# Deformable attention and bottleneck on one Trainium2 core: a different order in the stretch before the first image's attention

## The chip, the cores and the metric

The kernel runs on one core of one Trainium2 chip. The metric is the device time of that core in microseconds. A core has five engines that run their own instruction queues and meet only at semaphores: TensorE (PE, with its weight loads PEld), VectorE (DVE), ScalarE (ACT), GpSimd (POOL) and SyncE (SP), which here issues most of the DMA transfers. Each queue is worked off in the order in which the program wrote it, so an instruction that waits holds back everything behind it on its own engine.

## The reference, cut to what matters

The input `x` is 8 images of 512 channels and 64 by 64 pixels, in fp32. Layer 0 is deformable attention on the group-normalised input, layer 1 a convolutional bottleneck on the group-normalised sum. The part that matters here is the beginning of layer 0:

```python
x = x + _L0_conv_ref(_gn(x), w_q, w_off1, b_off1, w_off2, w_kv, w_out, b_out)
...
q = einsum('oc,bchw->bohw', w_q, x)                 # 512 x 512 weights
t = gelu(oi[:, :, ::4, ::4] * w_off1 + b_off1)      # every 4th pixel of q
off = tanh(einsum('oc,bchw->bohw', w_off2, t)) * 4.0
kv_feats = grid_sample_bilinear(oi, vgrid)          # 256 points, gathered from q itself
k, v = split(einsum('oc,bchw->bohw', w_kv, kv_feats), 2)
attn = softmax(einsum('bhid,bhjd->bhij', q * scale, k))   # 8 heads of 64, 256 keys
```

So an image goes through statistics, normalisation, query projection `q`, offsets, a gather of 4 neighbours of each sample point out of `q`, the keys and values of the 256 sampled points, and then the attention proper.

## The kernel before, in words

**Tiling.** An image lies in SBUF as 8 tiles of 512 pixels; a tile is 128 partitions by 4 channel blocks by 512 pixels, 1 MB. `x_tile`, `q_tile` and `out_tile` are neighbouring places in one region, so `q` of tile t overwrites the place of x tile t-1. Two regions hold two images at a time.

**Statistics** (`norm_x`, `group_stats`, `norm_q`). `bn_stats` (L201) runs on DVE per tile and channel block as the tiles land. Then `group_stats` has a short chain with no other work beside it: 4 `bn_aggr` (L169, DVE), a product `gps` with the group matrix in `cst` (L173, PE), 4 small DVE instructions (L175 to L179), a second product `gpsb` (L182, PE), `ve` (L184, DVE) and the power -0.5 on POOL (L185). The functions are generators: every `yield` hands control back to the caller, who decides what is written into the queues in between. After that `normalise` (L217, L221) scales x in place: tile 0 on DVE, tile 1 on POOL, tiles 2 to 7 on ACT with the bias `shift` (L230).

**Query projection** (`project_q`). A Strassen-like scheme with 7 half-size products per tile replaces 8. The weight sums (`of_weights`, L253 to L259) and the pixel sums (`of_tile`, L264 to L270) are made on DVE. A `product` is 8 PE instructions (4 fp32 matmuls, two passes each) with 256 moving columns. Per tile the order is p1 and p2, p6, p7, p5, p4, p3, and after each the DVE additions that bring the result out of PSUM: p6 to L364 and p2 to L365, p7 to L372, p5 to L378, p4 to L385 and p5 to L386, p3 to L391. p1, p2 and p7, p4 sit in pairs of banks of pool `ps_s`; p6, p5, p3 take single banks of `ps_mm`, which has two, so each of them needs the bank of the second last user to be free. `by_pixel` (L324 to L335) transposes the finished tile before, copies it (`qr`) and stores it to DRAM (`qd`), from where it is gathered later. For the last tile there is no next tile to hide in: its four transposes come after the last product, their copies go to DVE (L332), and `qr` of image 1 has two buffers.

**Sampling** (`sample`). Offsets by 8 small products `po` for each half (L424, one bank of `ps_mm`), tanh on ACT (L433), some 25 small DVE instructions in three groups, and then 20 slots. 16 of the slots issue two indirect gathers on POOL each (L519); 8 of them, three slots after the first gathers of their half step, also weigh what has landed (L483 to L488, DVE); two transpose the finished features into channels (`to_channels`, L493 and L498, one bank of `ps_mm`).

**What sets the order here.** Everything inside `manual_schedule` is queued in program order. At the start: `load_x(0)`, `load_wq`, `load_x(1)` and more on SP; statistics and normalisation of image 0; `project_q` of image 0, into whose steps the statistics of image 1 are dealt. Then `project_q` of image 1 and `sample` of image 0 are interleaved (L1193 to L1200): each sampling step adds to `room` (6 for a slot, 2 for one of the three steps before), and steps of `project_q` are taken while `room` is positive, each subtracting the number it yields (4, 2.5, 2.5, 2.5, 2.5, 2 per tile). After that: the last four transposes of image 1 (`drain(other)`), `next(samples[1])` (the `po` products and tanh of image 1), the load of `wout`, `project_k(0)` (4 banks of 8 PE instructions, each scaled into `kt` by ACT at L540, then a maximum over `kt` on DVE, L546), the first `logits`, `project_v(0)` (L560), and the attention loop over 8 images of 8 tiles of 4 head pairs.

Of the kernel before, what the change touches and what calls it, by code (L numbers as in the profile page):

```python
# [8 lines left out]
F32 = mybir.dt.float32  # L9
I32 = mybir.dt.int32  # L10
AF = mybir.ActivationFunctionType
ALU = mybir.AluOpType
# [4 lines left out]
P = 128  # L17
# [5 lines left out]
TP = 512  # L23
NT = N // TP
# [25 lines left out]
def kernel(  # L50
# [15 lines left out]
    nc = tc.nc  # L66
# [8 lines left out]
    ps_a = ctx.enter_context(tc.tile_pool(name="ps_a", bufs=1, space=PSUM))  # L75
# [6 lines left out]
    wbuf = cpool.tile([P, NCC, TP], F32, name="wbuf")  # L82
# [18 lines left out]
    def x_tile(b, t):  # L101
        return spot(b, t + 1)
# [8 lines left out]
    ident = cpool.tile([P, P], F32, name="ident")  # L111
    make_identity(nc, ident)
    cst = cpool.tile([P, K_N], F32, name="cst")
    nc.sync.dma_start(cst, consts)
    vec = cpool.tile([P, V_N], F32, name="vec")
    nc.sync.dma_start(vec, vecs)
    nhalf = cpool.tile([P, NCC], F32, name="nhalf")
    nc.vector.memset(nhalf, -0.5)

# [14 lines left out]
    def load_wq():  # L134
        nc.sync.dma_start(wbuf, w_qT.rearrange("(cc p) o -> p cc o", p=P))
# [19 lines left out]
    def drain(*gens):  # L155
        for gen in gens:
            for _ in gen:
                pass
# [30 lines left out]
    LATE = 0.01  # L189
# [4 lines left out]
    def load_x(b, order=range(NT), queue=nc.sync):  # L194
        for t in order:
            queue.dma_start(x_tile(b, t), xs[place[b]][:, :, t * TP : (t + 1) * TP])
# [7 lines left out]
    def quarters(a):  # L204

        h = C // 2
        return [[a[:, 2 * i : 2 * i + 2, h * j : h * (j + 1)] for j in range(2)] for i in range(2)]

    def norm_q(b, st, norms):

        gs = yield from group_stats(st, 0, b)
        shift = small.tile([P, NCC], F32, tag="shift", name=f"shift_{b}")

        def normalise(t, cc):
            xc, scale = x_tile(b, t)[:, cc, :], gs[:, 1, cc : cc + 1]
            if t < 2:
                (nc.vector, nc.gpsimd)[t].tensor_scalar(  # L217
                    xc, xc, gs[:, 0, cc : cc + 1], scale, ALU.subtract, ALU.mult
                )
            else:  # L220
                nc.scalar.activation(  # L221
                    xc, xc, AF.Identity, bias=shift[:, cc : cc + 1], scale=scale
                )

        norms[b] = normalise
        yield None
        for t in (1, 0):
            for cc in range(NCC):
                normalise(t, cc)
        nc.vector.scalar_tensor_tensor(shift, gs[:, 0], -1.0, gs[:, 1], ALU.mult, ALU.mult)  # L230
        yield None

    def project_q(b, normalise, mq, qd, pools, sums, aside=None):

# [7 lines left out]
        s1, s2, s4, t1, t2_, first = sums  # L242
# [1 line left out]

        (w11, w21), (w12, w22) = quarters(wbuf)
        V = nc.vector

        def of_weights(n):

            if b == 1:  # L250
                return
            if n == 1:
                V.tensor_add(s1, w21, w22)  # L253
            elif n == 2:
                V.tensor_sub(s2, s1, w11)
            elif n == 3:
                V.tensor_sub(w21, w11, w21)
            else:
                V.tensor_sub(s4, w12, s2)  # L259

        def of_tile(t, n):
            (x11, x12), (x21, x22) = quarters(x_tile(b, t))
# [75 lines left out]
            )  # L338

        for n in range(1, 4):  # L340
            of_weights(n)
            of_tile(0, n)
        for t in range(NT):
            (x11, x12), (x21, x22) = quarters(x_tile(b, t))
            (q11, q12), (q21, q22) = quarters(q_tile(b, t))

            def pixels(k):

                if t:
                    by_pixel(t - 1, k)  # L350
                if t + 2 < NT:
                    normalise(t + 2, k)

            bank1, bank2 = two_banks(t, 0)
            p1 = product(bank1, w11, x11)
            p2 = product(bank2, w12, x21)
            nc.scalar.copy(q11, p1)
            of_tile(t, 4)
            if t:
                activate(t - 1)  # L360
            yield 4
            p6 = product(one_bank(t, 1), s2, t2_)
            pixels(0)
            V.tensor_add(q12, q11, p6)  # L364
            V.tensor_add(q11, q11, p2)  # L365
            if t == 0:
                of_weights(4)
            yield 2.5
            bank1, bank2 = two_banks(t, 2)
            p7 = product(bank1, w21, x12)  # L370
            pixels(1)
            V.tensor_add(q22, q12, p7)  # L372
            if aside and t in (3, 4):
                largest(2, t - 3)
            yield 2.5
            p5 = product(one_bank(t, 3), s1, t1)
            pixels(2)
            V.tensor_add(q12, q12, p5)  # L378
            if t + 1 < NT:
                of_tile(t + 1, 1)  # L380
                of_tile(t + 1, 2)
            yield 2.5
            p4 = product(bank2, w22, x21)
            pixels(3)
            V.tensor_add(q21, q22, p4)  # L385
            V.tensor_add(q22, q22, p5)  # L386
            if t + 1 < NT:
                of_tile(t + 1, 3)
            yield 2.5
            p3 = product(one_bank(t, 4), s4, x22)  # L390
            V.tensor_add(q12, q12, p3)  # L391
            if t == 2 and aside:
                aside()
            elif t + 1 < NT:
                largest(t, 0)
                largest(t, 1)
            yield 2
# [129 lines left out]
    def project_k(b, mq, w=None):  # L527

        feats = feats_of(b)
        for oc in range(NCC):  # L530
            pk = ps_mm.tile([P, TP], F32, tag="mm", name=f"pk_{b}_{oc}")
            for cc in range(NCC):
                nc.tensor.matmul(  # L533
                    pk[:, :NK],
                    (w[cc // 2][:, cc % 2] if w else wbuf[:, cc])[:, oc * P : (oc + 1) * P],
                    feats[:, cc // 2, cc % 2, :],
                    start=(cc == 0),
                    stop=(cc == NCC - 1),
                )
            nc.scalar.mul(kt[:, oc, :], pk[:, :NK], SCALE)  # L540
        if w is None:
            load_wkv(1)

        if mq is not None:
            mk = small.tile([P, 2, NCC], F32, tag="mk", name=f"mk_{b}")
            nc.vector.tensor_reduce(  # L546
                mk[:, 0, :], kt, axis=AX.X, op=ALU.max, apply_absolute_value=True
            )
            nc.vector.tensor_reduce(
                mk[:, 1, :], mq.rearrange("p t c -> p c t"), axis=AX.X, op=ALU.max  # L550
            )
            nc.vector.tensor_mul(bounds[:, b, :], mk[:, 0, :], mk[:, 1, :])
# [17 lines left out]
    exps, sums = {}, {}  # L570

    def logits(b, t, hp):
        qt = q_tile(b, t)
        es = exps[b, t, hp] = []
        for kc in range(2):
            ps = ps_s.tile([P, 2, TP], F32, tag="s", name=f"ps_{b}_{t}_{hp}_{kc}")
            for a in range(2):
                r = DH * a
                for k in (0, DH):
                    nc.tensor.matmul(  # L580
                        ps[k : k + DH, a, :],
                        kt[r : r + DH, hp, kc * P + k : kc * P + k + DH],
                        qt[r : r + DH, hp, :],
                        start=True,
                        stop=True,
                    )
            e = free_es.pop(0)
            nc.scalar.activation(e, ps, AF.Exp)  # L588
            es.append(e)
# [515 lines left out]
    names = [(b, t, hp) for b in range(B) for t in range(NT) for hp in range(NCC)]  # L1105
    st1s, mqs = {}, {}
# [43 lines left out]
    norms = {}  # L1150
# [17 lines left out]

    with tc.manual_schedule():
        load_x(0)  # L1170
        load_wq()
        load_x(1)

        wkv = [es4[0:2], es4[2:4]]
# [5 lines left out]
        st = new_stats(0, 0)  # L1180
        drain(norm_x(0, st))

        shared = [wout[:, i, :].rearrange("p (k o) -> p k o", k=2) for i in range(3)]
        shared += [kt[:, 0:2, :], kt[:, 2:4, :], wout[:, 3, :]]
        drain(norm_q(0, st, norms))

        st = new_stats(0, 1)
        blocks, other = norm_x(1, st), norm_q(1, st, norms)
# [4 lines left out]
        other = make_q(1, shared)  # L1193
        next(other)
        rest.pop(0)()
        room = 0
        for step in samples[0]:
            room += 6 if step is None else 2
            while room > 0:
                room -= next(other, 6) or 6  # L1200
        drain(other)
        rest.pop(1)()
        next(samples[1])
        load_wout()
        project_k(0, mqs.pop(0), wkv[0])
        logits(*names[0])
        project_v(0, wkv[1])
        for g in range(len(names)):
            b, r = divmod(g, ROUNDS)
# [56 lines left out]
        b, t, st = B - 1, NT - 1, st1s.pop(B - 1)  # L1266
# [10 lines left out]
        for hp in range(NCC):  # L1277
            for a in range(2):
# [5 lines left out]
                    start=True,  # L1284
# [127 lines left out]
```

## Time and profile before

| | us |
|---|---|
| median of 3 runs (lowest, highest) | 3277.78 (3276.54, 3277.90) |
| the profiled execution, its own time | 3278.57 |
| its span, first to last instruction | 3276.8 |
| PE busy in the span | 3209.6 (98%) |
| DVE, ACT, POOL busy | 2325.3, 1188.6, 614.0 |

The stretch that the change touches, by busy time of the engines in stretches of 20 us:

| stretch, us | PE | DVE | ACT | POOL | what runs |
|---|---|---|---|---|---|
| 0 to 20 | 0.00 | 12.31 | 1.28 | 0.69 | x of image 0 lands, statistics |
| 20 to 40 | 7.46 | 16.68 | 0.68 | 7.84 | statistics end, first products |
| 40 to 140 | 100.00 | 88.27 | 40.98 | 3.75 | q of image 0 |
| 140 to 160 | 17.95 | 16.17 | 5.62 | 10.00 | end of q 0, start of q 1 |
| 160 to 260 | 97.60 | 81.67 | 37.62 | 31.94 | q of image 1, samples of image 0 |
| 260 to 280 | 17.80 | 7.79 | 3.65 | 0.00 | end of q 1, keys of image 0 |
| 280 to 300 | 19.43 | 4.28 | 9.87 | 0.00 | values, first attention rounds |

A row of the timeline reads: start, duration of the merged group, engine, line, operation, output, inputs, shape, how often; in brackets the idle time of the engine before it and what released it. PE busy is modelled from pipelined matmuls.

### The profile page before, as it was taken

Reading aid. Unit: us, or ns where it says so; the run is one execution under the profiler, and the core shown is the slowest. Engines: PE = TensorE matmul, PEld = TensorE weight load, DVE = VectorE, ACT = ScalarE, POOL = GpSimd, SP = SyncE. Lnnn points to the kernel's source line nnn. Section 1 sums busy time; section 2 is a strip of 40 time slices with the busy share of each in tenths; the row PEclk is TensorE's granted clock in tenths of the full one; section 3 lists DMA queues with packets and bytes.
Section 4 is the critical chain, followed back from the end, with each engine's and each line's share of the span. In section 5 each row is a group of like instructions: output and inputs, shape, how many; then the busy total and the mean of one; then the engine's idle time right before and its main releaser. Section 6 shows DMA issues by size and latency. Waiting matters only on the chain.

```text
span 3276.8 us, 46318 instructions
## 1 busy us (share of the span) xinstructions
PE 3209.6 (98%) x18256; PEld 1535.1 (47%) x18256; DVE 2325.3 (71%) x3781; ACT 1188.6 (36%) x1652; POOL 614.0 (19%) x579
## 2 busy tenths in 40 slices
PE   6999999999999999999999999999999999999997
PEld 5884223348332583326833267322763228533223
DVE  7884765787757868587775977669776687766565
ACT  2343333344333443234333443334432354332530
POOL 1130300140402304022040220303112040210301
PEclk9999999999999999999999999999999999999998
DMA  7232221572326623275332843238332482322713
GB/s 276 78 92 77 78 78 65 194 158 75 116 91 204 132 78 117 78 228 120 91 92 98 224 114 110 86 128 199 93 106 82 168 193 68 107 93 68 130 40 143
DMA packets 293858, 390.60 MB, mean 119 GB/s; under 512 B 18312, under 2 KB 157832, under 8 KB 293632
## 3 DMA queue, kind: packets, MB, share of 16 engines
q1 hardware_dynamic: 240352, 261.70, 24.4%
q0 software_dynamic: 53280, 125.86, 17.3%
q8 instruction: 145, 2.38, 0.3%
q14 instruction: 81, 0.66, 0.1%
HBM read 193.52 MB, written 192.94 MB: 118 GB/s over the span
## 4 chain that ended last, share of the span: by engine, by line
PE 94%; DVE 3%; issue 1%; ACT 0%; DMA 0%; SPq 0%; POOL 0%; ACTq 0%; DVEq 0%; POOLq 0%
PE pp L667 27%; PE pq L275 23%; PE ps L580 14%; PE pa L598 13%; PE pqt L324 4%; PE pn L625 4%; PE pk L533 2%; PE pv L560 2%; PE po L1003 2%; PE py L733 1%; DVE rn L638 1%; DVE image L1090 0%; PE po L424 0%; PE pu L930 0%; DVE st L201 0%
## 5 line engine op out<-in xcount | busy, mean ns | idle before, releaser
L667 PE MATMUL pp<-image,wout 128*64 128x512 f32 x3584 | 818.6, 599 | 0.2 <-DVE qr L332 0.2
L588 ACT ACTIVATE es<-ps 128x1024 f32<-128x1024 f32 x512 | 502.6, 1023 | 259.4 <-PE ps L580 209.0
L598 PE MATMUL pa<-es,vt 128*64 128x512 f32 x2048 | 489.1, 598 | 1.7 <-ACT es L588 1.7
L667 PEld LDWEIGHTS pp<-image,wout 128*64 128x64 f32 x3584 | 236.9, 136 | 541.1 <-issue 463.7
L275 PE MATMUL pq<-image,wbuf 128*128 128x256 f32 x2048 | 476.4, 381 | 3.3 <-DVE image L217 1.9
L519 POOL DMA_INDIRECT g<-qd,row x256 | 281.1, 1098 | 1056.0 <-DVE row L516 990.5
L580 PE MATMUL ps<-image,kt 64*64 64x512 f32 x3584 | 437.3, 602 | 0.3
L275 PEld LDWEIGHTS pq<-image,wbuf 128*128 128x128 f32 x2048 | 382.0, 191 | 56.1 <-issue 5.0
L676 DVE SCALAR_TENSOR_TENSOR image<-pp,vec,image 128x512 f32<-128x512 f32 x224 | 167.2, 746 | 333.0 <-PE pp L667 332.6
L605 ACT COPY image<-pa 128x512 f32<-128x512 f32 x224 | 132.1, 590 | 675.7 <-PE pa L598 675.7
L610 DVE TENSOR_TENSOR es<-es,es 128x1024 f32<-128x1024 f32 x256 | 311.0, 1215 | 71.4 <-PE pa L598 71.4
L598 PEld LDWEIGHTS pa<-es,vt 128*64 128x64 f32 x2048 | 137.4, 137 | 294.7 <-issue 274.8
L580 PEld LDWEIGHTS ps<-image,kt 64*64 64x64 f32 x3584 | 114.4, 132 | 307.4 <-issue 175.7
L334 ACT COPY qr<-pqt 128x512 f32<-128x512 f32 x224 | 131.2, 586 | 238.1 <-PE pqt L324 225.4
L638 DVE RECIPROCAL rn<-pn 128x512 f32<-128x512 f32 x63 | 211.3, 3354 | 7.7 <-PE pn L625 5.8
L651 DVE STREAM_SHUFFLE rb<-rn 128x512 f32<-128x512 f32 x252 | 184.6, 732 | 0.1
L185 POOL TENSOR_TENSOR gs<-ve,nhalf 128x4 f32<-128x4 f32 x15 | 15.6, 1042 | 895.6 <-DVE ve L184 895.6
L275 PE MATMUL pq<-es,es 128*128 128x256 f32 x768 | 181.5, 379 | 0.0
L1055 POOL DMA_DIRECT2D out_dram<-part x126 | 138.0, 1323 | 153.9 <-ACT part L1050 146.6
L201 DVE BATCH_NORM_STATS2 st<-image 128x6 f32<-128x512 f32 x256 | 159.2, 678 | 7.5 <-DMA image<-in_x_dram 7.3
L679 DVE BATCH_NORM_STATS2 st<-image 128x6 f32<-128x512 f32 x224 | 155.6, 694 | 7.7
L653 DVE TENSOR_TENSOR image<-image,rb 128x512 f32<-128x512 f32 x220 | 152.5, 693 | 7.6
(231 smaller groups left out, 3509.1 us busy)
## 6 DMA issues: line engine op xcount, KB each, us to landing
qd<-qr SPq DMA_DIRECT2D x256, 256.0 KB
image<-in_x_dram SPq DMA_DIRECT2D x112, 512.0 KB
out_dram<-image SPq DMA_DIRECT2D x49, 1024.0 KB
image<-in_x_dram POOLq DMA_DIRECT2D x48, 1024.0 KB, 10.3
out_dram<-part POOLq DMA_DIRECT2D x126, 256.0 KB, 7.2
image<-in_x_dram SPq DMA_DIRECT2D x16, 1024.0 KB
wbuf<-in_w_kvT_dram SPq DMA_DIRECT2D x14, 1024.0 KB
out_dram<-spare POOLq DMA_DIRECT2D x56, 256.0 KB, 8.0
```

What stands on the lines that cost most here:

```text
L201: nc.vector.bn_stats(st[:, cc, t, :], x_tile(b, t)[:, cc, :])
L275: nc.tensor.matmul(bank[:, o * 2 * P : (o + 1) * 2 * P], w[:, k, o * P : (o + 1) * P], xh[:, k, :], start=(k == 0), stop=(k == 1),)
L519: nc.gpsimd.indirect_dma_start(held[-1][:, i, :, :].rearrange("p j d -> p (j d)"), None, qd[:, :], bass.IndirectOffsetOnAxis(ap=row[:, ky, ...
L580: nc.tensor.matmul(ps[k : k + DH, a, :], kt[r : r + DH, hp, kc * P + k : kc * P + k + DH], qt[r : r + DH, hp, :], start=True, stop=True,)
L588: nc.scalar.activation(e, ps, AF.Exp)
L598: nc.tensor.matmul(pa[a * DH : (a + 1) * DH, :], vt[:, kc, hd * DH : (hd + 1) * DH], es[kc][:, a, :], start=(kc == 0), stop=(kc == 1),)
L610: nc.vector.tensor_add(es[0], es[0], es[1])
L638: nc.vector.reciprocal(rn, denominators.pop((b, t)))
L651: nc.vector.stream_shuffle(rb, rn, [2 * (hp % 2) + hp // 2] * 32)
L667: nc.tensor.matmul(pp[r : r + DH, :], wout[:, hp, oc * P + r : oc * P + r + DH], ao[:, hp, :], start=(hp == 0), stop=(hp == NCC - 1),)
L676: nc.vector.scalar_tensor_tensor(xt[:, oc, :], pp, col(V_BOUT + oc), xt[:, oc, :], ALU.add, ALU.add)
L679: nc.vector.bn_stats(st[:, oc, t, :], xt[:, oc, :])
```

## The change

It touches only what is queued before the attention loop. Six edits:

1. The loads of `cst` and `vec` move on SP from ahead of the eight loads of x to behind them, ahead of `load_wq`.
2. `of_weights` becomes a function of its own. For image 0, n = 1 is queued on DVE after the four small instructions of `group_stats`, and n = 2 after `ve`; n = 3 and 4 stay where they were. Image 1 makes none, as before.
3. `keep_up(5)` queues five fp32 products of `ident` with x tile 6 (512 columns) on PE ahead of `gps`, and `keep_up(2)` two more after `gpsb`; nothing reads their result.
4. `normalise` of image 0, tile 0, channel blocks 2 and 3 goes to ACT; `shift` is made between block 1 and block 2 of tile 0 rather than after block 3, for every image.
5. The dealing of samples: a slot now adds 4.5 and one of the three steps before it 5.
6. `project_q` of image 1 is run up to its mark `LATE` (before the last four transposes), then `project_k(0)` is queued, then the transposes, the maxima, `logits`, then `next(samples[1])`, the load of `wout` and `project_v(0)`.

```diff
     cst = cpool.tile([P, K_N], F32, name="cst")
-    nc.sync.dma_start(cst, consts)
     vec = cpool.tile([P, V_N], F32, name="vec")
-    nc.sync.dma_start(vec, vecs)
...
-            if t < 2:
+            if t == 1 or t == 0 and (b or cc < 2):
                 (nc.vector, nc.gpsimd)[t].tensor_scalar(
...
         for t in (1, 0):
             for cc in range(NCC):
+                if t == 0 and cc == 2:
+                    nc.vector.scalar_tensor_tensor(
+                        shift, gs[:, 0], -1.0, gs[:, 1], ALU.mult, ALU.mult
+                    )
                 normalise(t, cc)
-        nc.vector.scalar_tensor_tensor(shift, gs[:, 0], -1.0, gs[:, 1], ALU.mult, ALU.mult)
         yield None
+
+    def of_weights(n, sums):
+
+        s1, s2, s4 = sums[:3]
+
+        (w11, w21), (w12, w22) = quarters(wbuf)
+        if n == 1:
+            nc.vector.tensor_add(s1, w21, w22)
+        elif n == 2:
+            nc.vector.tensor_sub(s2, s1, w11)
+        elif n == 3:
+            nc.vector.tensor_sub(w21, w11, w21)
+        else:
+            nc.vector.tensor_sub(s4, w12, s2)
...
         for n in range(1, 4):
-            of_weights(n)
+
+            if b not in (0, 1) or (b == 0 and n == 3):
+                of_weights(n, sums)
             of_tile(0, n)
...
-            if t == 0:
-                of_weights(4)
+            if t == 0 and b != 1:
+                of_weights(4, sums)
...
         load_x(0)
+        nc.sync.dma_start(cst, consts)
+        nc.sync.dma_start(vec, vecs)
         load_wq()
...
-        drain(norm_q(0, st, norms))
+
+        idle = ps_a.tile([P, TP], F32, tag="pa", name="idle")
+
+        def keep_up(n):
+            for _ in range(n):
+                nc.tensor.matmul(idle, ident, x_tile(0, NT - 2)[:, 0, :], start=True, stop=True)
+
+        keep_up(5)
+        steps = norm_q(0, st, norms)
+        next(steps)
+        next(steps)
+        of_weights(1, shared)
+        next(steps)
+        of_weights(2, shared)
+        drain(steps)
+        keep_up(2)
...
         for step in samples[0]:
-            room += 6 if step is None else 2
+            room += 4.5 if step is None else 5
             while room > 0:
                 room -= next(other, 6) or 6
+        while next(other) != LATE:
+            pass
+        project_k(0, mqs.pop(0), wkv[0])
         drain(other)
         rest.pop(1)()
+        logits(*names[0])
         next(samples[1])
         load_wout()
-        project_k(0, mqs.pop(0), wkv[0])
-        logits(*names[0])
         project_v(0, wkv[1])
```

More of the change, by code (lines that the diff above doesn't have):

```diff
@@ L246, in project_q @@
         V = nc.vector
[L248 to L259, printed above, removed]
         def of_tile(t, n):
```

## The prediction

> **What bounds the kernel now.** I read the page's chain first, for the engine on which time counts.
>
> ```profile
> PE 94%; DVE 3%; issue 1%; ACT 0%; DMA 0%; SPq 0%; POOL 0%; ACTq 0%; DVEq 0%; POOLq 0%
> ```
>
> PE sets the end. So an edit is worth the PE idle time, or slow PE time, that it takes out of the first 300 us, provided PE stays the limit behind it; from about 290 us the attention loop is untouched and moves as a block. Next the timeline of the start (start, duration, group; in brackets idle time and releaser):
>
> ```profile
> 1.67 13.04 SPq L196 DMA_DIRECT2D image<-in_x_dram  x8
> ...
> 26.26 2.47 DVE L201 BATCH_NORM_STATS2 st<-image 128x6 f32<-128x512 f32 x4 [0.24 <-DMA image<-in_x_dram]
> ...
> 29.75 0.59 PE L173 MATMUL gps<-mv,cst 128*128 128x4 f32 x2 [29.75 <-DVE mv L169]
> ...
> 31.80 0.16 DVE L184 TENSOR_SCALAR ve<-gpsb 128x4 f32<-128x4 f32 x1 [0.68 <-PE gpsb L182]
> 32.05 1.03 POOL L185 TENSOR_TENSOR gs<-ve,nhalf 128x4 f32<-128x4 f32 x1 [30.74 <-DVE ve L184]
> 33.11 2.71 DVE L217 TENSOR_SCALAR image<-image,gs 128x512 f32<-128x512 f32 x4 [1.15 <-POOL gs L185]
> ...
> 33.72 5.56 PE L275 MATMUL pq<-image,wbuf 128*128 128x256 f32 x16 [1.95 <-DVE image L217]
> ...
> 39.12 1.89 PE L275 MATMUL pq<-kt,wout 128*128 128x256 f32 x8
> ```
>
> DVE follows the landing of x; then one chain runs to PE's first product. The 16 instructions of p1 and p2 take 39.12 - 33.72 = 5.40 us, where later groups of 8 follow each other by 1.73 us (0.216 each, so 3.46 for 16). In between they come every 0.427 us: PE starts at half speed. From 39.12 PE runs without a gap to 144. The same view later, only where PE waits between 160 and 290 us:
>
> ```profile
> 162.26 1.99 PE L275 MATMUL pq<-image,wbuf 128*128 128x256 f32 x8 [1.33 <-DVE spare L372]
> ...
> 221.62 1.99 PE L275 MATMUL pq<-image,wout 128*128 128x256 f32 x8 [1.06 <-DVE image L386]
> ...
> 264.99 1.99 PE L275 MATMUL pq<-image,wout 128*128 128x256 f32 x8 [0.77 <-ACT image L498]
> ...
> 272.06 2.90 PE L533 MATMUL pk<-image,es 128*128 128x256 f32 x8 [0.29 <-ACT pos L433]
> ...
> 275.44 5.91 PE L533 MATMUL pk<-image,es 128*128 128x256 f32 x24 [0.47 <-ACT kt L540]
> ...
> 283.16 7.13 PE L560 MATMUL pv<-es,image 128*128 128x512 f32 x16
> ...
> 290.22 1.94 PE L598 MATMUL pa<-es,vt 128*64 128x512 f32 x8
> ```
>
> And busy time in stretches (PE, PEld, DVE, ACT, POOL, then granted clock): the keys run while the clock is down.
>
> ```profile
> 272.00:276.00 4.00, 3.46 (x9) 2.38 (x10) 3.30 (x4) 0.40 (x2) 0.00 (x0) 0.62 0.62 149
> ```
>
> [...]0.427 against 0.216 us, with the turn about 3.6 us after 33.72. [...]after 15 transposes and 16 four-column products (267.77 to 271.8) the clock is 0.62. [...]tanh at 836.1 after the exp table's load at 827.99 and no further load until 1131.2. [...]L264 takes 1.09 us beside POOL at 36.4 and 0.69 later.
>
> **Start, step by step.** *Loads.* `cst` and `vec` are issued at 0.74 and 1.22, x at 1.67; x now goes at 0.74, 0.93 earlier. x stays limited by its transfer (a tile per 2.7 us), so the last tile lands at 25.33. Behind it come cst and vec (106 KB, an estimated 0.3 to 0.7 us at 385 GB/s or somewhat less), needed by `gps` at 28.82, and wbuf (2.7 us, by about 28.8), needed by n = 1 at about 30.0: covered by 1 to 3 us. SP issues wbuf at the same 14.75 as before, so later loads aren't late. -0.93.
> *Idle products.* Tile 6 lands at 22.62 (23.55 before). Five products are 10 instructions of 512 columns: 0.854 cold, 0.432 warm. With 3.6 us cold, 4.2 of them go cold and 5.8 warm: 6.1 us, end 28.7, against `gps` at 28.82. `gps` is queued right behind them; if the turn comes 0.7 us later it is late by about 0.3. Two more (4 x 0.432 = 1.73) fill 30.4 to 32.1, before the first product at 32.6.
> *Sums in the gaps.* n = 1 (0.68) on DVE covers the 0.68 in which `ve` waits for `gpsb`; with a warm PE `gpsb` returns sooner, so DVE becomes the last to end: together -0.16. n = 2 (0.68) lies in the 1.15 us of the power[...]: 0 to +0.6, no row shows the pair; I take +0.3 as the middle. Without it `normalise` starts at 32.02 (-1.09).
> *First products.* Blocks 0 and 1 on DVE end at 33.4, shift at 33.5, blocks 2 and 3 on ACT (2.93 / 4, about 0.75 each) at 34.3 and 35.0, where DVE had them at 35.8. p1 runs 32.63, waits for block 1, ends 34.7; p2 (block 3 for its second half) 36.43. `t1` and `t2_` on DVE end at 35.7 to 36.1. So p6 starts at 36.43: 39.12 - 36.43 = 2.69, minus 0.3 = **2.4**. Of it 1.9 is PE's clock and 0.9 the loads, less what the waits for blocks return. POOL's four of tile 1 (10.56 us) end by about 42.7; `of_tile(1, 2)` asks for them at 43.1, a cover of 0.4. For image 1 shift moves inside the same DVE sequence: 0.
>
> **Dealing.** Going through both lists of yields gives the order. *Tile 0*: before, the eight small instructions for `pos` (1.72 us on DVE) stood between p6's and p7's additions, and p4 waited for L372 1.33 us. Now they come after L372, which ends at 160.6 in the old clock, when p5 ends (160.8). The other small groups (1.3 and 1.0 us) now stand behind tile 0's p4 and tile 1's p1, p2; with them L372 of tile 1 ends at 174.4, just when p4 wants its bank: 0.15 lost. Gain 1.2. *Transposes to channels*: before, both stand between p4 and p3 and take p3's bank in turn, so that p3 waits for L386 (1.06) and for L498 (0.77). Now they stand after tile 4's p6 and tile 6's p7; the next to take a bank is p5, whose bank is free since L364. Gain 1.06 + 0.77 = 1.83; their own 0.47 each only moves. *Denser gathers*: from second gathers to weighing there are now 7.5 to 11 units of 0.87 us. Row cast behind other DVE work, two gathers (1.25 each), and landing
>
> ```profile
> DMA to landing us min/median/max: 2.4/2.7/3.4
> ```
>
> leave 0.1 to 2 us on the narrowest (half steps 5 and 6), and DVE has 0.4 us to p4's bank after that. Cost 0 to 0.5, taken 0. DVE carries 9.9 us per tile (11 x 0.69 + 2.35) and at most 3 us of sampling in 13.97. **3.0** in all.
>
> **Keys ahead.** Before: last p3 ends at 264.99 + 1.99 = 266.98; first `pa` at 290.22: 23.24 us. After, from the end of p3: keys 32 x 0.216 = 6.91, warm and without the waits (ACT scales a bank within 0.4, two banks ahead); transposes 4 x 0.47 to 8.8; logits 1.95 to 10.75; po 1.96 to 12.7. `pv` then needs the `ps_mm` bank of the last transposes. On DVE the maximum over `kt` is queued ahead of the copies and waits for the fourth scaling: 7.35 + 1.22 + 0.2 + 0.16 = 8.95; copies at 8.95 and 9.65; the third and fourth wait for the stores of the first two (about 2.45 from copy's end to release, as from 269.2 to 271.67): the fourth ends at 13.5. `pv` starts at 13.55 and takes 7.06: 20.6. Gain 23.24 - 20.6 = **2.6**. exp and kt are done long before. The four stores and the loads of wbuf and wout behind them on SP go out within 1 us of where they did; `wout` is wanted at 321.9 and the gathers of image 1 at 325.
>
> **Sum.** 2.4 + 3.0 + 2.6 = 8.0 us. The profiled execution would have 3278.57 - 8.0 = 3270.6 with a span of 3268.8; it lies 0.79 above the median of the runs, so the median becomes 3277.78 - 8.0 = 3269.8. What a measurement of this kernel can tell from no change is 0.2%, 6.56 us: faster means below 3271.2.
>
> **Rivals.**
> 1. *The clock falls in the moved tail.* [...]if the clock is down for pv, 3.6 us at half speed cost 1.8, and logits a few tenths: the tail gives 0.5, in all 5.9: 3271.9. For it: 272 to 276 above. Against: 1.95 us of logits stand between, and each quiet stretch is shorter than the 4 us that brought the clock down. The same total comes if the fuller DVE takes back the 1.2 of tile 0 and part of the waits for banks.
> 2. *Idle products too long.* All five cold are 8.54 us, from 22.62 to 31.16; `gps` is 2.34 late, two more cold ones take 3.41 us to about 36.3, and p6 starts at 41.7: a loss of 2.6 instead of 2.4 gained: 3274.8. Against: the first dense stretch turned after 3.6 us.
> 3. *Slower: DVE waits for gathers.* `weigh` stands ahead of the additions on DVE; if landing takes over some 5.5 us instead of 2.7, each of eight costs PE about 1.85, 14.8 in all, against 8.0 gained: 3284.6. It decides from 14.6 us, the gain and 6.6 more. Against: 3.4 at most so far, and the DMA engines are 0.23 to 0.41 busy from 160 to 260.
> 4. *The change does less because the gain is paid back later.* PE has no wait for DMA or x of later images in its chain, so I see no place and give it no chance of its own.
>
> **How the numbers follow.** Forecast 0.60, its own range 3268.3 to 3271.6, about 0.04 of it above the bound; rival 1 0.22; rival 2 0.10; rival 3 0.05; a little more gain (no wait for pv's bank[...]: 9.2, 3268.6, and less) 0.03. Faster 0.56 + 0.03 = 0.59; same 0.04 + 0.22 + 0.10 = 0.36; slower 0.05. The range takes in the forecast and rival 1 with its bounds and leaves out rivals 2 and 3: 3267.0 to 3274.5.
>
> **What would show it.** x's first issue at 0.74; `normalise` at about 32.2 and p6 at about 36.7; no PE wait on L372 in tile 0 of image 1 and none on L386 or L498; keys in 6.9 us with clock 1.00; first `pa` near 282.2 in place of 290.22. It is wrong if `gps` starts after 29.5, if L483 waits for DMA, or if pv's instructions come every 0.85 us.

## The result, and the profile after

| | before | after |
|---|---|---|
| median, us (lowest, highest; 20 runs each) | 3277.77 (3276.15, 3279.37) | 3272.61 (3267.79, 3273.63) |
| profiled execution, own time | 3278.57 | 3273.27 |
| its span | 3276.8 | 3271.5 |

The ratio is 0.9982, with a 95% interval of 0.9976 to 0.9988: 5.16 us less in the median, where 8.0 were forecast. The time lies inside the range on record, but under the 0.2% that was set as the bound of faster. The runs after spread over 5.8 us, those before over 3.2 here and over 6.2 in a later set of 39 (3273.76 to 3279.95), so the spread need not come from the change.

The gain is best read at three places: the start of p6 of image 0, the start of the last p3 of image 1, and the first `pa` of the attention loop.

| from, to (start of the PE group) | before | after | gained | forecast |
|---|---|---|---|---|
| 0 to p6 of image 0 | 39.12 | 37.59 | 1.53 | 2.4 |
| p6 of image 1 to its last p3 | 155.51 to 264.99: 109.48 | 153.98 to 259.60: 105.62 | 3.86 | 3.0 |
| last p3 of image 1 to first `pa` | 264.99 to 290.22: 25.23 | 259.60 to 285.34: 25.74 | -0.51 | 2.6 |
| together | 290.22 | 285.34 | 4.88 | 8.0 |

(Between p6 of image 0 and p6 of image 1 nothing moved: 155.51 - 153.98 is again 1.53.) The other 0.4 us of the span's 5.3 lie behind the first `pa`, where nothing was changed; what makes them up stays open. The page of the changed kernel still names PE:

```profile
PE 95%; DVE 3%; issue 1%; ACT 1%; DMA 0%; POOL 0%; SPq 0%; ACTq 0%; DVEq 0%; POOLq 0%
```

**Start.** The timeline of the changed kernel, to be laid beside that of before (L194 answers to L196, L171 to L173, L183 to L185, L215 to L217, L277 to L275):

```profile
0.74 12.17 SPq L194 DMA_DIRECT2D image<-in_x_dram  x8
...
22.31 6.04 PE L1196 MATMUL idle<-image,ident 128*128 128x512 f32 x10 [22.31 <-DMA image<-in_x_dram]
...
28.38 0.39 PE L171 MATMUL gps<-mv,cst 128*128 128x4 f32 x2
...
30.19 0.69 DVE L242 TENSOR_TENSOR wout<-wout,wbuf 128x512 f32<-128x512 f32 x1
30.31 1.46 POOL L183 TENSOR_TENSOR gs<-ve,nhalf 128x4 f32<-128x4 f32 x1 [29.00 <-DVE ve L182]
...
31.80 1.38 DVE L215 TENSOR_SCALAR image<-image,gs 128x512 f32<-128x512 f32 x2 [0.92 <-POOL gs L183]
...
33.32 1.28 ACT L219 ACT_TABLE_LOAD   x1 [33.32 <-DVE shift L228]
34.61 1.52 ACT L219 ACTIVATE image<-image,shift,gs 128x512 f32<-128x512 f32 x2
35.48 2.27 PE L277 MATMUL pq<-image,wbuf 128*128 128x256 f32 x8 [0.69 <-ACT image L219]
...
37.59 1.89 PE L277 MATMUL pq<-kt,wout 128*128 128x256 f32 x8
```

The statistics of the last tile start 1.37 us earlier, the short products return faster (`gps` takes 0.39 us instead of 0.59), the power on GpSimd takes 1.46 us instead of 1.03, and DVE starts to normalise at 31.80, 1.31 earlier. Then comes a line that was not there before: ScalarE loads its activation table at 33.32, between `shift` and the two scalings that p2 waits for. Before, the first load stood at 0.74 in front of an idle engine.

**Dealing.** In the changed kernel no PE group between 149 and 261 us waits: the three waits shown before (1.33, 1.06, 0.77) have no successor.

**Tail.** The timeline and the stretches (PE, PEld, DVE, ACT, POOL, granted clock) of the changed kernel:

```profile
261.33 7.11 PE L537 MATMUL pk<-image,es 128*128 128x256 f32 x32
...
268.27 2.06 PE L326 MATMUL pqt<-ident,image 128*128 128x128 f32 x16
...
270.27 1.95 PE L584 MATMUL ps<-spare,kt 64*64 64x512 f32 x16
...
272.15 1.06 PE L428 MATMUL po<-vec,wout 128*128 128x4 f32 x8
...
275.26 10.15 PE L564 MATMUL pv<-es,image 128*128 128x512 f32 x16 [1.16 <-DVE qr L334]
...
285.34 1.94 PE L602 MATMUL pa<-es,vt 128*64 128x512 f32 x8
```

```profile
275.20:279.00 3.80, 3.74 (x5) 1.68 (x6) 2.25 (x3) 0.00 (x0) 0.00 (x0) 0.50 0.92 244
279.00:283.00 4.00, 4.00 (x8) 1.60 (x7) 0.00 (x0) 0.58 (x1) 0.00 (x0) 0.71 1.04 387
```

The keys now run in 7.11 us, with a granted clock of 1.00. But the values, which took 7.13 us before, now take 10.15, with the granted clock at 0.50 and then 0.71. This is one execution; more of them stand under the clock in the tail.

### The profile page after: what moved, and what is told of

It reads as the page before. It is cut to its first block, busy times and chain, and to the rows that moved or that the text cites. A ratio compares the mean times of both kernels' runs of the same rounds, so it can differ in the third digit from the quotient of the medians.

```text
span 3271.5 us, 46349 instructions
## 1 busy us (share of the span) xinstructions
PE 3216.1 (98%) x18270; PEld 1536.2 (47%) x18270; DVE 2322.9 (71%) x3779; ACT 1189.5 (36%) x1654; POOL 613.4 (19%) x579
## 4 chain that ended last, share of the span: by engine, by line
PE 95%; DVE 3%; issue 1%; ACT 1%; DMA 0%; POOL 0%; SPq 0%; ACTq 0%; DVEq 0%; POOLq 0%
PE pp L671 27%; PE pq L277 24%; PE ps L584 14%; PE pa L602 13%; PE pn L629 4%; PE pqt L326 4%; PE pv L564 2%; PE pk L537 2%; PE po L1007 2%; PE py L737 1%; DVE rn L642 1%; DVE image L1094 0%; PE po L428 0%; DVE st L199 0%; PE pu L934 0%
## 5 line engine op out<-in xcount | busy, mean ns | idle before, releaser
L277 PE MATMUL pq<-image,wbuf 128*128 128x256 f32 x2048 | 475.3, 380 | 1.4 <-ACT image L219 0.7
L277 PEld LDWEIGHTS pq<-image,wbuf 128*128 128x128 f32 x2048 | 380.5, 191 | 55.0 <-issue 5.0
L183 POOL TENSOR_TENSOR gs<-ve,nhalf 128x4 f32<-128x4 f32 x15 | 16.1, 1070 | 893.6 <-DVE ve L182 893.6
L277 PE MATMUL pq<-es,es 128*128 128x256 f32 x768 | 181.5, 379 | 0.0
```

The source lines that it names most:

```text
L277: nc.tensor.matmul(bank[:, o * 2 * P : (o + 1) * 2 * P], w[:, k, o * P : (o + 1) * P], xh[:, k, :], start=(k == 0), stop=(k == 1),)
```

## The experiments

Each is the changed kernel with one edit, unless said otherwise. My theory after the result: the start is short by the table load, the tail by PE's clock, and the dealing gains at the three places named in the forecast. The rivals stand with each run. Where a single edit was timed more than once, the interval of its ratio overlaps with that of the changed kernel, so each conclusion on one edit rests on times between two marks in a profile, and a median is given beside it.

### The table load

```diff
         load_x(0)
+        scratch = small.tile([P, NCC], F32, tag="scratch", name="scratch")
+        nc.scalar.copy(scratch, nhalf)
```

> The changed kernel with one more instruction: a copy of 4 columns on ScalarE at the start, so that the activation table is loaded before anything waits. Theory (the start gained 1.5 us instead of 2.4 because the table load of 1.28 us moved from 0.74 us into the chain, behind the wait for shift): the two scalings on ScalarE end near 34.8 instead of 36.1, p6 starts at 36.5 to 36.7 instead of 37.59, the time falls by 0.9 to 1.1 us. Rival (the first products are late for VectorE's or the clock's sake): p6 stays at 37.4 to 37.6.

Measured: 3269.05 us in the median (3267.78 to 3271.86, 7 runs), ratio to the kernel before 0.9974 (0.9963 to 0.9985). From this kernel's timeline:

```profile
32.16 1.38 DVE L215 TENSOR_SCALAR image<-image,gs 128x512 f32<-128x512 f32 x2 [0.92 <-POOL gs L183]
...
33.70 1.52 ACT L219 ACTIVATE image<-image,shift,gs 128x512 f32<-128x512 f32 x2 [31.47 <-DVE shift L228]
...
36.72 1.89 PE L277 MATMUL pq<-kt,wout 128*128 128x256 f32 x8
```

From the start of L215 to p6 it takes 36.72 - 32.16 = 4.56 us, against 37.59 - 31.80 = 5.79 in the changed kernel: 1.23 less, close to the 1.28 of the table load. The theory holds. The first `pa` came 2.19 us earlier (283.15 instead of 285.34): 0.87 from p6, since x landed 0.36 later here, and 1.32 because the values took 8.83 us instead of 10.15. The median fell by 3.2 to 3.6 us against two measurements of the changed kernel, where 0.9 to 1.1 were expected; the table load explains 1.23 of it, and the rest stays open.

### The clock in the tail

Values straight behind the keys:

```diff
         project_k(0, mqs.pop(0), wkv[0])
+        project_v(0, wkv[1])
         drain(other)
         rest.pop(1)()
         logits(*names[0])
         next(samples[1])
         load_wout()
-        project_v(0, wkv[1])
```

> The changed kernel with project_v(0) queued straight behind project_k(0), ahead of the last transposes, the logits and po. Theory (the values lost 3.1 us because PE's clock had fallen in the quiet 3 us before them, po and the wait for the last transposes' copy): values in 6.9 us at full clock, first pa 19.8 us after the end of the last p3 instead of 23.9, so 4.1 us less in the median than the changed kernel, near 3268.5. If the clock now falls before pa instead, 2 us less only. Rival (the values are slow for another reason, such as the loads of wbuf and wout beside them): values still take 10 us, time within 1 us of the changed kernel.

Measured: 3269.61 (3267.83 to 3270.56, 8 runs), ratio 0.9973 (0.9962 to 0.9983). In its timeline:

```profile
260.89 1.89 PE L277 MATMUL pq<-image,wout 128*128 128x256 f32 x8
262.62 7.11 PE L537 MATMUL pk<-image,es 128*128 128x256 f32 x32
269.56 7.03 PE L564 MATMUL pv<-es,image 128*128 128x512 f32 x16
...
282.18 1.94 PE L602 MATMUL pa<-es,vt 128*64 128x512 f32 x8
```

The same 16 instructions take 7.03 us, and the way from the last p3 to `pa` is 21.29 instead of 25.74: 4.45 less, as expected. The median is only 3.0 less than that of the changed kernel; in this profile the start was 1.3 us later (p6 at 38.87), for the reason shown under the idle products.

The maxima behind the copies, so that the wait before the values shrinks while their place stays:

```diff
-        project_k(0, mqs.pop(0), wkv[0])
-        drain(other)
+        project_k(0, mqs.pop(0), wkv[0], lambda: drain(other))
...
+        if late:
+            late()
         if mq is not None:
             mk = small.tile([P, 2, NCC], F32, tag="mk", name=f"mk_{b}")
```

> The changed kernel with the maxima over kt (L550 to L556) queued on VectorE behind the copies of the last transposes instead of ahead of them, so that the copies end earlier and the values wait less. Theory (the quiet stretch of 3.1 us, po and the 1.16 us wait, lets the clock fall): the wait goes from 1.16 to under 0.2 us, the quiet stretch to 2 us, the values run warm in 7 us: 4 us less, near 3268.6. Rival (po's four-column products alone, 2 us, bring the clock down): only the wait is saved, 1.1 us, and the values still take 10 us.

Measured: 3270.91 (3266.96 to 3272.37, 13 runs), ratio 0.9978 (0.9970 to 0.9986). The profiled execution was the fastest of them:

```profile
275.68 7.13 PE L566 MATMUL pv<-es,image 128*128 128x512 f32 x16 [0.21 <-DVE qr L334]
```

Here the wait is 0.21 and the values take 7.13 us again, as before ("warm"). That does not show that the shorter wait kept them warm. There are six profiles in which the values stand behind `po` and a wait of 1.14 to 1.16 us. In five of them the values took 8.55 to 10.15 us. In the sixth, the second kernel of the places in the dealing below, they were warm with the full wait:

```profile
277.04 7.13 PE L564 MATMUL pv<-es,image 128*128 128x512 f32 x16 [1.14 <-DVE qr L334]
```

There the way from the last p3 to `pa` took 22.71 us, 2.52 less than before. So the same order of products loses the clock in some executions and not in others.

Nor is the time of the execution with the late maxima, 3266.96, a time of the tail alone. Its first `pa` starts at 282.74, 2.6 us earlier than that of the changed kernel, but its span is 6.5 us shorter. Nearly all of the other 3.9 lies in one stretch near the end, which no edit touches. The same view of the changed kernel and of this one (last before the DMA share and GB/s: the granted clock):

```profile
3224.00:3252.00 28.00, 21.64 (x127) 12.37 (x128) 17.20 (x41) 5.16 (x9) 5.21 (x5) 0.82 0.29 108
...
3224.00:3252.00 28.00, 22.07 (x144) 10.33 (x142) 21.56 (x46) 6.82 (x11) 8.89 (x7) 1.00 0.52 196
```

In the profile of before the clock fell there too, to 0.82. Over the whole span this execution was granted 0.998, the twelve other profiled ones 0.995 or 0.996. The median, 1.5 us less than that of the changed kernel, lies between the rival (1.1 less) and the theory (4 less), and one profile cannot tell them apart. What the shorter wait is worth stays open.

Edit 6 undone, the tail of before behind the new dealing:

```diff
-        while next(other) != LATE:
-            pass
-        project_k(0, mqs.pop(0), wkv[0])
         drain(other)
         rest.pop(1)()
-        logits(*names[0])
         next(samples[1])
         load_wout()
+        project_k(0, mqs.pop(0), wkv[0])
+        logits(*names[0])
         project_v(0, wkv[1])
```

> The changed kernel with edit 6 undone (transposes, po, then keys, logits, values), everything else kept. Theory: edit 6 is worth nothing in the median, since it moves the loss of clock from the keys to the values: from the end of the last p3 to pa 23.2 us as before against 23.9, so the time is that of the changed kernel or up to 0.7 us less, 3271.9 to 3272.6. The forecast's step (edit 6 gains 2.6 us): 3275.2.

Measured: 3271.96 (3267.04 to 3273.47, 21 runs), ratio 0.9981 (0.9975 to 0.9988). The lines that show where the clock is lost now:

```profile
266.76 2.88 PE L537 MATMUL pk<-image,es 128*128 128x256 f32 x8 [0.29 <-ACT pos L437]
270.12 5.93 PE L537 MATMUL pk<-image,es 128*128 128x256 f32 x24 [0.47 <-ACT kt L544]
...
277.85 7.13 PE L564 MATMUL pv<-es,image 128*128 128x512 f32 x16
284.92 1.94 PE L602 MATMUL pa<-es,vt 128*64 128x512 f32 x8
```

From the last p3 (259.79) to `pa` 25.13, against 25.74 with edit 6. Undoing the edit costs nothing here. What edit 6 saves at the keys, their slow clock and three waits, it loses at the values, if the clock falls there as in the profile of the changed kernel. Over the six profiles above the way from the last p3 to `pa` took 22.71 to 25.74, so edit 6 gave between +2.5 and -0.5 us against before, and the forecast's 2.6 lies at the upper end. The medians (3271.96 against 3272.61 and 3272.24) show no gain.

### The idle products

```diff
-        keep_up(5)
         steps = norm_q(0, st, norms)
...
         drain(steps)
-        keep_up(2)
```

> The changed kernel without the seven idle products. Theory (their gain is small, since ScalarE's table load holds p2 back to 35.5 anyway, and in some executions the first five end after the statistics and hold gps back by 1.2 to 1.4 us): gps, gpsb return 0.35 us later, p1 runs at half clock to about 36.4, p6 starts near 38.2 to 38.5 instead of 37.6 to 38.95; the time lies within 0.8 us of the changed kernel, either way. The forecast's step (1.9 us of the start's gain is PE's clock): 1.9 us more, 3274.5.

Measured: 3271.30 (3269.70 to 3273.51, 14 runs), ratio 0.9982 (0.9974 to 0.9990): the changed kernel's ratio without any idle product. In its profile p6 starts at 38.28, 0.69 later than in the changed kernel's profile. Why the median doesn't follow is to be seen in how long the same ten instructions take in other executions; the line of the kernel with the late maxima, and its `gps`:

```profile
22.42 7.58 PE L1198 MATMUL idle<-image,ident 128*128 128x512 f32 x10 [22.42 <-DMA image<-in_x_dram]
...
27.40 1.04 DVE L167 BATCH_NORM_AGGREGATE mv<-st 128x2 f32<-128x48 f32 x4
29.84 0.28 PE L171 MATMUL gps<-mv,cst 128*128 128x4 f32 x2
```

The means were ready at 28.44 and `gps` started at 29.84: the idle products held it back by 1.4 us. Over the seven profiles with the first five idle products on tile 6 and the table load in the chain, these five took 5.95 to 7.58 us, and p6 started at 37.59 to 38.95, later where they took longer, but for the shortest two. That is rival 2 of the forecast, in part and in some executions.

### The places in the dealing

```diff
-            room += 4.5 if step is None else 5
+            room += 5 if step is None else 2
```

> The changed kernel with 5 for a slot and 2 for a step before (then the group of eight small instructions stands again between p6's and p7's additions of tile 0, and both transposes to channels stay at places that take no bank from p3: behind tile 4's p1 and p2, and behind tile 6's p7). Theory: p4 of tile 0 of image 1 waits 1.3 us for L376 again and nothing for L390; from p6 of tile 0 to the end of the last p3 the way is 1.3 to 1.7 us longer than in the changed kernel (107.37 us from 154.12 to 261.49). Rival (dealing gains by its evenness, not by this one place): under 0.5 us longer.

One execution, 3275.73 us. From its timeline, p4 of tile 0 of image 1:

```profile
161.62 1.99 PE L277 MATMUL pq<-image,wbuf 128*128 128x256 f32 x8 [1.25 <-DVE spare L376]
```

The wait is back, the only one in the stretch, and from p6 (154.94) to the last p3 (262.09) it takes 107.15, 1.53 more than 105.62. One execution is enough for this stretch: in the ten profiles with the dealing of the changed kernel it took 105.62 us nine times and 105.70 once.

```diff
-            room += 4.5 if step is None else 5
+            room += 5.25 if step is None else 5
```

> The changed kernel with 5.25 for a slot and 5 for a step before: the group of eight stays behind p7's addition, the first transpose to channels stands behind tile 4's p4 again, the second behind tile 7's p7. Theory: p3 of tile 4 waits 1.06 us for L390 as before, and no other product waits; the way from p6 of tile 0 to the end of the last p3 is 1.1 us longer (108.5). Rival: no wait, since the gathers are less dense: 107.4.

One execution, 3271.55 us.

```profile
218.96 1.99 PE L277 MATMUL pq<-image,wout 128*128 128x256 f32 x8 [1.07 <-DVE image L390]
```

p3 of tile 4 waits for its bank again; from p6 (154.44) to the last p3 (261.39) 106.95, 1.33 more. In both kernels the gathers are less dense than in the changed one and the total is longer: it's the place of two groups that counts, not the evenness. What is left of the 3.86 us, 1.0, is put down to the second transpose to channels (0.77 of wait before); no run moves that one alone.

### A version that takes the parts that work

Four edits on the changed kernel: the table loaded early and the values behind the keys, as in the two diffs above, and these two, which put a sum behind `normalise`, and seven idle products on tile 5 in place of five on tile 6:

```diff
-        of_weights(2, shared)
         drain(steps)
+        of_weights(2, shared)
...
-        def keep_up(n):
+        def keep_up(n, t=NT - 2):
...
-                nc.tensor.matmul(idle, ident, x_tile(0, NT - 2)[:, 0, :], start=True, stop=True)
+                nc.tensor.matmul(idle, ident, x_tile(0, t)[:, 0, :], start=True, stop=True)
...
-        keep_up(5)
+        keep_up(7, NT - 3)
```

> The changed kernel with four edits: the table loaded at the start, of_weights(2) queued behind normalise (and so not beside the power on GpSimd), seven idle products on tile 5 instead of five on tile 6, and the values straight behind the keys. Theory: the power takes 1.05 us instead of 1.46; the idle products end before 28.4 in every execution; p6 starts at 36.0 to 36.4; the tail from the last p3 to pa takes 19.6 us; 1.3 + 4.3 us less than the profiled execution of the changed kernel: 3267 to 3268, and a spread of under 2 us. If only the clock's phase moved the loss, 3269 to 3271 with the same spread of 5 us.

Measured: 3266.73 (3265.74 to 3269.71, 5 runs), ratio 0.9966 (0.9952 to 0.9979). Here 3267 to 3268 with a spread of under 2 us were expected; the spread is 4. The profiled execution was the slowest and shows the early idle products failing:

```profile
19.93 7.67 PE L1198 MATMUL idle<-image,ident 128*128 128x512 f32 x14 [19.93 <-DMA image<-in_x_dram]
...
30.39 3.76 PE L1198 MATMUL idle<-image,ident 128*128 128x512 f32 x4
30.82 1.03 POOL L183 TENSOR_TENSOR gs<-ve,nhalf 128x4 f32<-128x4 f32 x1 [29.50 <-DVE ve L182]
```

They end at 27.6, and at 30.4 PE is slow again: the second group, four instructions of two products, takes 3.76 us instead of 1.96 and holds the first product to 33.95. The expectation that they'd end in time was right, and in this execution it didn't help. The power takes 1.03 us once no sum runs beside it, as in the next two kernels.

So the same with no idle products; on the changed kernel, beside the table and the values as above:

```diff
-        keep_up(5)
...
-        of_weights(2, shared)
         drain(steps)
-        keep_up(2)
+        of_weights(2, shared)
```

> The kernel of e_best without any idle products. Theory (what idle products gain by a warm clock they lose by holding gps back or by falling cold again before the first product): within 1 us of e_best5 and e_best's 3266.73, so 3266 to 3268; p6 at 37.4 to 38.0 in every execution. Rival (a warm start is worth 1.9 us): 3268.6.

And with the idle products as in the changed kernel, five and then two on tile 6, so that beside the table and the values only the sum moves; the changed kernel itself was run again on the same chip:

```diff
-        of_weights(2, shared)
         drain(steps)
+        of_weights(2, shared)
```

> The changed kernel with the table loaded at the start, of_weights(2) behind normalise and the values straight behind the keys; the idle products stay as in the changed kernel, five on tile 6. Theory: p6 starts at 36.1 when the idle products end in time and up to 1.4 us later when they do not; the tail takes 19.6 us; 3266 to 3268.

> The changed kernel once more, beside these two on one chip. Theory: 3271.5 to 3273, that is 5 us above both, with values at 7 to 10 us and idle products at 5.9 to 7.6 us[...].

| kernel | median (lowest, highest), runs | ratio to before | p6 in the profile | last p3 to `pa` |
|---|---|---|---|---|
| no idle products | 3268.75 (3267.11, 3270.28), 8 | 0.9972 (0.9961 to 0.9982) | 39.26 | 21.30 |
| five on tile 6 | 3267.05 (3266.48, 3268.43), 6 | 0.9969 (0.9956 to 0.9981) | 35.96 | 21.29 |
| changed kernel again | 3272.24 (3268.56, 3273.48), 14 | 0.9981 (0.9973 to 0.9989) | 38.35 | 24.41 |

With the table out of the way p6 starts at 35.96 behind idle products that took 6.00 us, and the idle products are worth 1.7 us between the medians: the rival's size, not mine (p6 without them was at 39.26, later than I had expected). The intervals of the two ratios overlap, so that size is not certain. Both medians beat that of the changed kernel on the same chip, by 3.5 and 5.2 us; with five on tile 6, the slowest run (3268.43) was faster than the changed kernel's fastest there (3268.56). In all four profiles with the values straight behind the keys they took 7.03 us.

## Why the prediction was right and wrong

**Loads ahead: right.** The profile of the changed kernel has 1.37 us instead of 0.93. But over the twelve profiles with this order the statistics of the last tile start at 24.89 to 25.36, which is 0.90 to 1.37 before the 26.26 of the one profile of before. So the forecast lies at the low end. That the transfers of cst and vec, which stood ahead of x too, make up the difference is likely, not shown. The load of wbuf was issued at 16.85, not at the 14.75 of the forecast; nothing waited for it.

**Sums in the gaps: right.** The chain from `gps` to `normalise` was 3.42 us (31.80 - 28.38) against 3.36 before (33.11 - 29.75): what the faster products gave, the power took. For a slower power beside the sum n = 2 the forecast had 0.3, the middle of an estimate that no row backed; measured was 0.43 (1.46 against 1.03). In the nine profiles with the sum beside it the power took 1.40 to 1.46 us, in the four without 1.03; what in the pair costs the time was not shown. With the sum behind `normalise` (five on tile 6) the same chain took 3.00 (31.41 - 28.41).

**First products: this step failed.** I put the two scalings on ScalarE at 34.3 and 35.0 from their durations, and left out that they had become the engine's first instructions. The table load, 1.28 us, a term that the sum doesn't have, went behind the wait of the first of them. Being first is not enough for that: before, the engine's first work, a copy at 39.32, also had to wait, and its load stood at 0.74 all the same. In the changed kernel's trace a wait instruction of its own, for two semaphores, stands on ScalarE ahead of the load, from 5.92 to 33.28; before, no such instruction stood there, and the copy carried its one wait itself. I had asked only whether tanh needs a new table, not where the first load stands. The run with the early load gave 1.23 us back, and in that one execution p6 at 36.72 is where the forecast has it (39.12 - 2.4). Behind the table load the idle products were worth little: without them p6 came 0.69 us later in the profiles, and with the load out of the way 3.3 later (39.26 against 35.96), or 1.7 in the medians.

**Idle products: half right.** The arithmetic of 6.1 us for a 3.6 us cold stretch fits the 6.04 of this profile. But I took the cold stretch from one execution. In the nine profiles with 5.95 to 7.58 us for the same instructions the step from one of them every 0.85 us to one every 0.43 came an estimated 2.9 to 6.2 us after the first, by the weight loads in the timelines (at some 25.4 in the shortest, 28.6 in the longest), and the upper half holds `gps` back.

**Dealing: right, under-sized.** 3.86 instead of 3.0; the place of `pos` is 1.53, the first transpose 1.33, and the remaining 1.0 would be the second. I priced a wait at its idle time; each cost some 0.2 to 0.3 us more than the idle time that the row shows. The gathers' narrow slack held: no `weigh` of this stretch waited, with landings of up to 4.6 us.

**Keys ahead: this step failed in the profiled execution.** The wait was sized well: the values started 275.26 - 261.33 = 13.9 us after the first key product, where 13.55 was forecast. The 7.06 behind it was wrong: 10.15, since the clock fell (0.50, then 0.71). That is rival 1, with a larger cost: 3.1 us at the values where it had 1.8 and some tenths for the logits. Between the logits and the values lies a stretch of 3.1 us with nothing but four-column products and the wait, and I had held the 1.95 us of logits and the shortness of the stretch against the rival. With the values straight behind the keys they took 7.03. Where the values kept to 7.13 us in spite of the stretch, the step gained 2.52, near the forecast's 2.6; so what failed is that a full clock was counted on.

What decides between the two was not shown, nor which of the products ahead of the values lets the clock fall. In the traces of before and of the changed kernel the changes of the granted clock lie whole multiples of 3.41 us apart (before from 37.48 to 273.00, which is 69 of them, and one more to 276.41; in the changed kernel from 25.36 to 274.53, which is 73, and two more to 281.36). The stretch of 3.1 us is close to one such step in length. That its outcome hangs on how it lies to these steps would be an estimate from two traces, and no run tests it.

**The total: partly luck.** The median, 3272.61, lies inside the range because the range took in rival 1 (3271.9), and the forecast of faster by over 0.2% did not come in; "same" had 0.36. The parts are not those of rival 1: the start gave 0.87 less than forecast, for a reason that no rival named, the dealing 0.86 more, and the tail 3.1 less where rival 1 had 2.1. That the first two cancel is luck.

## What to carry to other kernels

When work moves to an engine that was idle so far, ask what its first instruction there brings along: a table load in front of it (1.28 us here) can stand behind that instruction's waits and count on the path, unless something harmless comes first. Behind a TensorE stretch of some 3 us with only tiny products and waits, slow products have to be reckoned with (8.55 to 10.15 us instead of 7.13 in five of six profiles here), and since it can differ from one execution to the next, one profile doesn't settle it; moving dense work next to dense work was safer here (values in 7.03 us in all four profiles) than filling gaps. Before a fast execution is put down to an edit, look whether the rest of its span ran as in the others. In a pool of two banks, what matters about a small extra user is between which two others it stands, and that can be read off the program before anything runs.

## What the runs showed of the hardware that was not expected

- The same ten dense fp32 instructions after a long idle time took 5.95, 6.00, 6.04, 6.26, 6.60, 7.01, 7.18, 7.42 and 7.58 us in nine profiles; the step from 0.85 to 0.43 us for each came an estimated 2.9 to 6.2 us after the first, by their weight loads.
- Behind the same 3.1 us of four-column products and a wait, the same 16 instructions took 10.15, 10.11, 8.83, 8.83, 8.55 and 7.13 us in six profiles.
- After 7.67 us of dense products, 2.8 us with only the two short products of the statistics (27.6 to 30.4) were enough, in one profile, for the next four instructions to take 3.76 us instead of 1.96.
- A GpSimd instruction on 4 columns took 1.40 to 1.46 us in nine profiles with one VectorE instruction of 0.68 to 0.69 us (the sum n = 2) beside it, and 1.03 in four without.
- With two loads of 106 KB together ahead of 8 MB, the work on the last of these started 0.90 to 1.37 us later than with the two behind (one profile against twelve).
